# An empty VectorE instruction ahead of each unit's product, more scan inputs made by TensorE, and a one-element minimum in another form

## The chip, the cores and the metric

The kernel runs on one core of one Trainium2 chip. The metric is the device time of one execution in microseconds (us); lower is better. Times given as a median come from three runs; the profile is of one further execution.

## What is computed

All arithmetic is in float32. The input `x` has 4 images of 384 channels and 32 x 32 positions (L = 1024). Layer 0 normalises over groups of channels and applies a four-direction selective scan; layer 1 is causal attention and a mixture of four experts with top-2 gates. The reference, cut to what matters here:

```python
# layer 0, per image and direction k (rows, columns, and both reversed)
x_dbl = einsum('bkdl,kcd->bkcl', xs, x_proj_weight)       # dts (12), Bs (16), Cs (16)
dt = softplus(einsum('bkrl,kdr->bkdl', dts, dt_projs_weight) + bias)
h = h * exp(dt * A) + (dt * u) * B                         # along l, 16 states for each channel
y = sum over states of h * C
x = x + gelu(layernorm(merge(y + D * u)))
# layer 1, tokens t of each image
t = t + softmax(causal(q k^T * scale)) v
t = t + sum over experts e of gate_e * (gelu(xn w1_e + b1_e) w2_e + b2_e)
```

## The kernel before, in words

The scan is cut into **units**: a unit is 32 channels x 4 states (128 partitions) by 1024 positions. An image has 192 units (3 blocks of channels, 4 directions, 4 sets of states, 4 parts of 32 channels), the kernel 768. Four units that follow each other (one set of states, all 128 channels) make a **group**. `IMAGE` is 192, `NJ` is 4, `NU` is 768.

A unit needs these steps, each by one helper:

- `decay` (L548, instruction at L552): ScalarE computes da = exp(dt * A). `dap` has three buffers, so the decay of unit n waits for the scan of unit n - 3.
- `front` (L556, L559): VectorE multiplies dt*u by B, both spread over 128 partitions in SBUF, and writes v to PSUM.
- `middle` (L561, L565): VectorE's scan h = h * da + v, with da in SBUF and v in PSUM. The pool of h has seven buffers.
- `back` (L570, L572): GpSimd multiplies h by C in place. It is given a dependency on the v product of the next unit, so that it runs beside a scan.
- `row` (L578, L597): TensorE sums the states of a group's four units into y by matmuls with a selection matrix.

In image 0, where TensorE has no attention or expert work yet, `feed` (L776) prepares some groups in another way: TensorE transposes dt*u (L815), ScalarE scales it by B (L838, 32 small instructions for a group), and `turned` (L852, L860) lets TensorE transpose the result into PSUM as v; such a unit has no `front`. `scaled` holds the prepared groups; the pool `st` has two buffers, and a group that would come too late is left out.

The order of all work is written by hand in one loop over a clock (L1393 on), one step per unit. In step t it issues the decay of unit t + 2, deferred work, `front(t)`, `turned(t + 1)`, `back(t - 1)`, more deferred work (`inner`), `middle(t)`, the row of the group that ended at t - 2, loads, a piece of the preparation of a coming image, and then TensorE work of attention and experts of an earlier image, with a budget of 4.4 us (attention) or 3.3 us (experts) for each step (`go_on`, L1364). Work is cut up by generators that yield ("wait", n) to go on n steps later, or ("pe", us) to charge their budget. Each engine runs its instructions in the order in which they were issued; a layer above adds the semaphore waits that the buffers need.

`preparation(b)` (L481) normalises an image and computes the projections; the preparation of image b + 1 runs beside the scan of image b, so those of images 0 and 1 fall in the steps of image 0. `project_dt` (L409) makes dt for two directions and one block of channels, in two halves of 512 positions: matmuls (L425), a step of waiting (L429), softplus on ScalarE (L431); then it stores dt to DRAM, multiplies by u on VectorE (L439) and stores the product.

`attention` (L942) handles 128 query rows at a time. `softmax` (L1008) takes the minimum over one or two pieces of the negated scores (L1014), combines two pieces with L1016, and lets ScalarE take the exponential (L1018); `normalise` (L1025) adds the two partial sums (L1028). `experts` (L1184) runs its matmuls at L1260 and L1285, moves the first to SBUF on ScalarE (L1245), applies gelu (L1249), and adds the second's result on VectorE (L1294, L1297), which frees its bank of PSUM.

The functions that the diff touches, and what calls them:

Of the kernel before, what the change touches and what calls it, by code (L numbers as in the profile page):

```python
# [10 lines left out]
ALU = mybir.AluOpType  # L11
# [22 lines left out]
NQ = N // NI  # L34
# [8 lines left out]
AHEAD = 5  # L43
# [6 lines left out]
def hybrid_kernel(  # L50
# [358 lines left out]
    def project_dt(b, pair, m, u, xd):  # L409

        ks = PAIRS[pair]
        while not slots.ready(3 + pair):
            yield "wait", 1
        v = u[m]
        if pair == 1:
            v = slots.now(f"ut_{b}_{m}", P, L)
            nc.scalar.copy(v.rearrange("p (w h) -> p w h", h=HW), columns(u[m]))
        dts = [slots.now(f"dt_{b}_{k}_{m}", P, L) for k in ks]
        for h in range(NH):
            while not banks.ready(2):  # L420
                yield "wait", 1
            pss = [banks.now(f"pdt_{b}_{k}_{m}_{h}") for k in ks]
            for i, k in enumerate(ks):
                r = slice(64 * pair + 32 * i, 64 * pair + 32 * i + R)
                nc.tensor.matmul(  # L425
                    pss[i], wdt[r, m * P : (m + 1) * P], xd[r, bass.ts(h, 512)],
                    start=True, stop=True,
                )
            yield "wait", 1  # L429
            for i, k in enumerate(ks):  # L430
                nc.scalar.activation(  # L431
                    dts[i][:, bass.ts(h, 512)], pss[i], AF.Softplus, bias=dtb[:, k, m : m + 1]
                )
                banks.give(f"pdt_{b}_{k}_{m}_{h}")
        yield "wait", 1
        for i, k in enumerate(ks):
            nc.sync.dma_start(dts_d[b, k][0, m * P : (m + 1) * P, :], dts[i])
            du = yield from slots.take(f"du_{b}_{k}_{m}", P, L)
            nc.vector.tensor_mul(du, dts[i], v)  # L439
            yield "wait", 1  # L440
            nc.sync.dma_start(dts_d[b, k][1, m * P : (m + 1) * P, :], du)
            if b == 0:
                stored_du.add((k, m))
            slots.give(f"dt_{b}_{k}_{m}", f"du_{b}_{k}_{m}")
        if pair == 1:
            slots.give(f"ut_{b}_{m}")
# [101 lines left out]
    def decay(n):  # L548
        u = units[n]
        u["da"] = dap.tile([P, L], F32, tag="da", name=f"da_{u['name']}")  # L550
        g = u["k"] * NG + u["m"] * NJ + u["j"]
        nc.scalar.activation(  # L552
            u["da"], spread["dt4", n], AF.Exp, scale=a4[:, g, u["q"] : u["q"] + 1]
        )

# [5 lines left out]
    def middle(n):  # L561
# [5 lines left out]
            op0=ALU.mult, op1=ALU.add,  # L567
        )

    def back(n, after):  # L570
        h = units[n]["h"]
        product = nc.gpsimd.tensor_tensor(h, h, spread["bc", n][:, 1, :], ALU.mult)  # L572
        order(product, after, mybir.DependencyClass.Sync, "beside a scan")

    ys = {}
# [2 lines left out]
    def row(n):  # L578

        u = units[n]  # L580
        b, m = u["b"], u["m"]
        first = u["pair"] == 0 and u["i"] == 0 and u["q"] == 0
        last = u["pair"] == 1 and u["i"] == 1 and u["q"] == NQ - 1
        if first:
            ys[b, m] = ps_y.tile([P, L], F32, tag="y", name=f"y_{u['name']}")
        for half in range(NH):
            for jj in range(NJ):
                h = units[n - NJ + 1 + jj]["h"]
                y = ys[b, m][jj * DJ : (jj + 1) * DJ, bass.ts(half, 512)]
                if u["pair"] == 0:  # L590
                    h = h[:, bass.ts(half, 512)]
                else:

                    h = h.rearrange("p (w h) -> p w h", h=HW)
                    h = h[:, :, half * HW // 2 : (half + 1) * HW // 2]
                    y = columns(y)
                nc.tensor.matmul(  # L597
                    y, sel, h, start=first, stop=last, tile_position=(0, jj * DJ)
                )
        if last:  # L600
            defer(2, lambda: evict(b, m), inner)
        elif u["pair"] == 1 and u["i"] == 1 and u["q"] == 0:
            side.append(skip(b, m))
# [172 lines left out]
    def feed():  # L776
        bt = one.tile([P, 2, NT, 4 * N], F32, tag="fx0", name="bt")

        def turn_rows(pair):
            while pair not in stored_rows:  # L780
                yield "wait", 1
            rows = yield from slots.take(f"bt_{pair}", 4 * N, L)
            nc.sync.dma_start(rows, rows_d[0, pair].rearrange("k j n l -> (k j n) l"))
            yield "wait", 2
            ps = yield from banks.take(f"pbt_{pair}")
            for t in range(NT):
                nc.tensor.transpose(
                    ps[:, t * 4 * N : (t + 1) * 4 * N], rows[:, t * P : (t + 1) * P],
                    ident[: 4 * N, : 4 * N],
                )  # L790
            yield "wait", 1
            nc.scalar.copy(bt[:, pair], ps.rearrange("p (t n) -> p t n", t=NT))
            banks.give(f"pbt_{pair}")
            slots.give(f"bt_{pair}")

        begun = []
        yield from turn_rows(0)
        for n in range(0, IMAGE, EACH):
            u = units[n]
            if clock[0] > n + EACH - NJ - AHEAD:  # L800
                continue
            if u["pair"] == 1 and u["m"] == 0 and u["i"] == 0:
                yield from turn_rows(1)
            while (u["k"], u["m"]) not in stored_du:
                yield "wait", 1
            name = f"turn_{u['name']}"
            du = yield from slots.take(name, P, L)
            nc.sync.dma_start(du, dts_d[0, u["k"]][1, u["m"] * P : (u["m"] + 1) * P, :])
            yield "wait", 2

            def dut(q, h, du=du, name=name):
                ps = banks.now(f"{name}_{q}_{h}")
                for t in range(4):
                    o = (4 * h + t) * P
                    nc.tensor.transpose(ps[:, t * P : (t + 1) * P], du[:, o : o + P], ident)  # L815
                return ps

            for q in range(1, NQ, 2):
                n0 = n + q * NJ
                if clock[0] > n0 - AHEAD:  # L820
                    continue
                while len(begun) >= 2 and clock[0] < begun[-2] + NJ:

                    yield "wait", 1
                if clock[0] > n0 - AHEAD:
                    continue
                begun.append(n0)
                st = pools["st"].tile([P, NT, NJ * P], F32, tag="st", name=f"st_{n0}")
                ps = [None, None]
                for h in range(2):  # L830
                    if ps[h] is None:
                        while not banks.ready():
                            yield "wait", 1
                        ps[h] = dut(q, h)
                        yield "wait", 1
                    for t in range(4):
                        for i in range(NI):
                            nc.scalar.activation(  # L838
                                st[:, 4 * h + t, :].rearrange("p (d i) -> p i d", i=NI)[:, i, :],
                                ps[h][:, t * P : (t + 1) * P], AF.Copy,  # L840
                                scale=bt[:, u["pair"], 4 * h + t, u["i"] * 2 * N + q * NI + i :][:, :1],
                            )
                        if t == 1:
                            if h == 0 and banks.ready():
                                ps[1] = dut(q, 1)
                            yield "wait", 1
                    banks.give(f"{name}_{q}_{h}")
                    yield "wait", 1
                scaled[n0] = st
            slots.give(name)  # L850
# [91 lines left out]
    def attention(b, yb, fx0):  # L942
# [65 lines left out]
        def softmax(i, ss, pr):  # L1008
# [4 lines left out]
            for n, (o, e, ps) in enumerate(ss):  # L1013
                nc.vector.tensor_reduce(nb[:, n : n + 1], ps, AX.X, ALU.min)  # L1014
            if len(ss) == 2:
                nc.vector.tensor_tensor(nb[:, 0:1], nb[:, 0:1], nb[:, 1:2], ALU.min)  # L1016
            for n, (o, e, ps) in enumerate(ss):
                nc.scalar.activation(  # L1018
                    pr[:, o:e], ps, AF.Exp, bias=nb[:, 0:1], scale=-1.0,
# [5 lines left out]
        def normalise(i, nb, n):  # L1025
            wd = (i + 1) * P
            if n == 2:
                nc.vector.tensor_add(nb[:, 2:3], nb[:, 2:3], nb[:, 3:4])  # L1028
            nc.vector.reciprocal(nb[:, 2:3], nb[:, 2:3])
            nc.scalar.activation(prs[i][:, :wd], prs[i][:, :wd], AF.Copy, scale=nb[:, 2:3])  # L1030

# [361 lines left out]
    while t < NU + 4 or waiting or side or due or inner or parked:  # L1393
# [5 lines left out]
        if t == IMAGE:  # L1399
            second()  # L1400
            side.append(fold())
        done = None
        if t < NU and "v" not in units[t]:
            done = front(t)
        if t + 1 < IMAGE:
# [71 lines left out]
```

## Time and profile before

| what | value |
| --- | --- |
| median of three runs | 3781.38 us (3779.78 to 3781.87) |
| profiled execution: time, span | 3782.19 us, 3780.4 us |
| mean granted TensorE clock | 0.926 |
| first scan of image 0, 1, 2, 3 starts at | 50.3, 682.9, 1511.4, 2331.6 us |
| last scan starts at | 3112.0 us |
| busy in the span: PE, DVE, ACT, POOL | 3348.6, 2962.4, 2088.0, 1815.4 us |
| L565 scan, 768 of them | 1750.6 us busy, 2284 ns each |
| L559 v product, 678 | 840.6 us busy, 1240 ns each |
| L572 product on GpSimd, 768 | 1814.3 us busy, 2367 ns each |
| L552 decay, 768 | 882.8 us busy, 1156 ns each |

PE is TensorE's matmuls and PEld its weight loads, DVE is VectorE, ACT ScalarE, POOL GpSimd, SP the queue that issues DMAs. A line like L565 is the line of the kernel that issued the instruction. The views used are: the page (busy shares, and 40 slices of the span with busy tenths), the timeline (start, duration, engine, line, operation, and in brackets the idle time in front with what ended it), groups of instructions by line (busy us, mean ns of one, idle in front), and tables of busy time in stretches. Ends of matmuls are modelled, and one profile entry stands for half of a program's float32 matmul.

### The profile page before, as it was taken

What the parts mean: (1) busy time and instruction counts of PE and PEld (TensorE: products, weight loads), DVE (VectorE), ACT (ScalarE), POOL (GpSimd) and SP (SyncE); (2) the same over time, 40 slices, a digit from 0 to 9 for tenths busy, and PEclk for the clock granted to TensorE, in tenths of its full rate; (3) what the DMA queues carried; (4) which work ended last, traced back from release to release, by engine and by line L of the source; (5) the groups of instructions that cost most, each with busy time, mean ns of one, the idle gap of its engine ahead of it and who ended that gap; (6) DMA issues with size and microseconds to landing.
All of it is one profiled execution on the core that took longest, in us unless ns stands there. A gap on an engine that the chain in (4) does not pass through costs nothing. (4 is left out here: it accounts for less than half of the span.)

```text
span 3780.4 us, 34707 instructions
## 1 busy us (share of the span) xinstructions
PE 3348.6 (89%) x11755; PEld 1523.6 (40%) x11755; DVE 2962.4 (78%) x2098; ACT 2088.0 (55%) x2754; POOL 1815.4 (48%) x776
## 2 busy tenths in 40 slices
PE   4666666689999999799999999889999998999999
PEld 1333323345343334345333344454344334644444
DVE  5899899988899899989988999999999992210000
ACT  5888888555666556556655555455554552322121
POOL 2777777545466556545555565455665660000000
PEclk7777876799999999898999999899999999999999
DMA  6656555635676757436666655455667551322321
GB/s 202 221 211 223 203 210 200 235 141 177 211 247 210 253 197 245 152 136 219 218 218 227 203 201 197 143 172 196 209 197 241 178 182 38 91 78 81 97 82 53
DMA packets 408017, 680.01 MB, mean 180 GB/s; under 512 B 33520, under 2 KB 279968, under 8 KB 407840
## 3 DMA queue, kind: packets, MB, share of 16 engines
q1 hardware_dynamic: 401632, 677.40, 52.6%
q8 instruction: 93, 1.52, 0.2%
q10 hardware_dynamic: 6208, 0.39, 0.1%
q14 instruction: 84, 0.69, 0.1%
HBM read 605.16 MB, written 72.55 MB: 179 GB/s over the span
## 5 line engine op out<-in xcount | busy, mean ns | idle before, releaser
L572 POOL TENSOR_TENSOR h<-h,bc 128x1024 f32<-128x1024 f32 x768 | 1814.3, 2367 | 1300.8 <-DVE v L559 1170.4
L565 DVE TENSOR_TENSOR_SCAN h<-da,v 128x1024 f32<-128x1024 f32 x768 | 1750.6, 2284 | 107.2 <-PE v L860 31.8
L552 ACT ACTIVATE da<-dt,a 128x1024 f32<-128x1024 f32 x768 | 882.8, 1156 | 916.0 <-DVE h L565 877.8
L1260 PE MATMUL ph<-fx,w 128*128 128x512 f32 x2304 | 1023.3, 600 | 3.5 <-DMA w<-in_w 2.0
L1285 PE MATMUL fy<-ht,w 128*128 128x512 f32 x2304 | 1022.4, 601 | 1.7 <-ACT dt L431 0.9
L559 DVE TENSOR_TENSOR v<-du,bc 128x1024 f32<-128x1024 f32 x678 | 840.6, 1240 | 35.0 <-DMA du<-dts 18.3
L1285 PEld LDWEIGHTS fy<-ht,w 128*128 128x128 f32 x2304 | 437.1, 192 | 575.9 <-issue 558.9
L1260 PEld LDWEIGHTS ph<-fx,w 128*128 128x128 f32 x2304 | 433.8, 191 | 578.6 <-issue 532.8
L597 PE MATMUL y<-h,sel 128*32 128x512 f32 x3072 | 489.7, 659 | 97.4 <-POOL h L572 97.2
L1245 ACT ACTIVATE ht<-ph,b1s 128x512 f32<-128x512 f32 x384 | 257.5, 678 | 463.3 <-PE ph L1260 462.5
L1294 DVE SCALAR_TENSOR_TENSOR fy<-fy,b2s,tw 128x512 f32<-128x512 f32 x96 | 72.4, 754 | 423.0 <-PE fy L1285 423.0
L597 PEld LDWEIGHTS y<-h,sel 128*32 128x32 f32 x3072 | 97.6, 116 | 407.4 <-issue 219.0
L860 PE MATMUL v<-ident,st 128*128 128x128 f32 x720 | 144.2, 366 | 112.7 <-DVE h L565 111.6
L838 ACT ACTIVATE st<-turn,bt 128x128 f32<-128x128 f32 x736 | 213.6, 532 | 0.1
L860 PEld LDWEIGHTS v<-ident,st 128*128 128x128 f32 x720 | 116.1, 190 | 158.3 <-DVE h L565 77.9
L1249 ACT ACTIVATE ht<-ht 128x3072 f32<-128x3072 f32 x64 | 176.9, 2764 | 0.8
L552 ACT ACT_TABLE_LOAD x108 | 138.6, 1283 | 15.5 <-DMA dt<-dts 11.8
L1067 PE MATMUL po<-pt,vt 128*128 128x256 f32 x480 | 110.2, 383 | 10.1 <-ACT pt L959 10.0
L425 PE MATMUL pdt<-xd,wdt 12*128 12x512 f32 x184 | 78.9, 753 | 33.4 <-ACT dt L431 24.7
L997 PE MATMUL ss<-axn,qt 128*128 128x512 f32 (+3 forms) x288 | 101.3, 497 | 7.7 <-ACT yb L1084 6.4
L1067 PEld LDWEIGHTS po<-pt,vt 128*128 128x128 f32 x480 | 96.0, 204 | 27.8 <-ACT pt L959 13.1
L997 PEld LDWEIGHTS ss<-axn,qt 128*128 128x128 f32 x288 | 50.5, 193 | 50.2 <-issue 30.0
(208 smaller groups left out, 1618.3 us busy)
## 6 DMA issues: line engine op xcount, KB each, us to landing
bc<-rows SPq DMA_DIRECT2D x384, 512.0 KB, 4.7
w<-in_w SPq DMA_DIRECT2D x384, 384.0 KB, 5.9
dt<-dts SPq DMA_DIRECT2D x192, 512.0 KB, 3.9
du<-dts SPq DMA_DIRECT2D x192, 512.0 KB, 6.5
dts<-dt SPq DMA_DIRECT2D x48, 512.0 KB, 3.6
dts<-du SPq DMA_DIRECT2D x48, 512.0 KB, 3.8
fx<-t2d SPq DMA_DIRECT2D x12, 768.0 KB, 5.8
tw<-mkd SPq DMA_DIRECT2D x32, 256.0 KB, 6.5
```

The costliest lines, as they stand in the source:

```text
L552: nc.scalar.activation(u["da"], spread["dt4", n], AF.Exp, scale=a4[:, g, u["q"] : u["q"] + 1])
L559: return nc.vector.tensor_tensor(u["v"], spread["du4", n], spread["bc", n][:, 0, :], ALU.mult)
L565: nc.vector.tensor_tensor_scan(u["h"][:, ::step], u["da"][:, ::step], u["v"][:, ::step], 0.0, op0=ALU.mult, op1=ALU.add,)
L572: product = nc.gpsimd.tensor_tensor(h, h, spread["bc", n][:, 1, :], ALU.mult)
L597: nc.tensor.matmul(y, sel, h, start=first, stop=last, tile_position=(0, jj * DJ))
L838: nc.scalar.activation(st[:, 4 * h + t, :].rearrange("p (d i) -> p i d", i=NI)[:, i, :], ps[h][:, t * P : (t + 1) * P], AF.Copy, scale=bt[ ...
L860: nc.tensor.transpose(u["v"][:, t * P : (t + 1) * P], st[:, t, u["j"] * P : (u["j"] + 1) * P], ident)
L1067: nc.tensor.matmul(pv[:, o:], vt[:, j, m * P : (m + 1) * P], pts[step][j // 4][:, j % 4, o:], start=(alone and j == 0), stop=(j == nj - 1),)
L1245: nc.scalar.activation(ht[:, f, :], ps, AF.Identity, bias=bias)
L1249: nc.scalar.activation(ht, ht, AF.Gelu)
L1260: nc.tensor.matmul(ps, tiles[n][:, c, (f % 2) * P : (f % 2 + 1) * P], xns[h][:, c, :], start=(c == 0), stop=(c == M - 1),)
L1285: nc.tensor.matmul(pss[m], tiles[n][:, f, :], hts[fh][:, f, :], start=(fh == 0 and f == 0), stop=(fh == 1 and f == FH - 1),)
```

## The change

Four edits.

1. In `project_dt`, the second half's step of waiting between matmul and softplus is left out while the clock is in image 0.
2. In `feed`, the groups prepared for TensorE are no longer every second one: of each five groups, numbered from the start of the image, those with remainder 1, 3 and 4 are.
3. The two combining instructions on one element for each partition (L1016, L1028) are written as tensor_scalar with the second operand as a per-partition scalar, in place of tensor_tensor.
4. From image 1 on, each step issues an empty VectorE instruction ahead of `front`. It is given dependencies on the unit's decay, and in the last unit of a group also on the product and the last row matmul of the unit four before. `decay`, `back` and `row` note their instructions for it.

```diff
@@ project_dt
-            yield "wait", 1
+            if h == 0 or clock[0] >= IMAGE:
+
+                yield "wait", 1
@@ decay
-        nc.scalar.activation(
+        u["decay"] = nc.scalar.activation(
@@ new, after middle
+    def ahead(n):
+
+        wait = nc.vector.engine_nop()
+        after = [units[n]["decay"]]
+        if n % NJ == NJ - 1 and n > NJ:
+
+            after += [units[n - NJ]["product"], units[n - NJ]["row"]]
+        for x in after:
+            order(wait, x, mybir.DependencyClass.Sync, "ahead of the product")
@@ back
-        product = nc.gpsimd.tensor_tensor(h, h, spread["bc", n][:, 1, :], ALU.mult)
+        product = units[n]["product"] = nc.gpsimd.tensor_tensor(h, h, spread["bc", n][:, 1, :], ALU.mult)
@@ row
-                nc.tensor.matmul(
+                units[n]["row"] = nc.tensor.matmul(
@@ feed
-            for q in range(1, NQ, 2):
+            for q in range(NQ):
                 n0 = n + q * NJ
-                if clock[0] > n0 - AHEAD:
+                if n0 // NJ % 5 not in (1, 3, 4) or clock[0] > n0 - AHEAD:
                     continue
@@ softmax
-                nc.vector.tensor_tensor(nb[:, 0:1], nb[:, 0:1], nb[:, 1:2], ALU.min)
+                nc.vector.tensor_scalar_min(nb[:, 0:1], nb[:, 0:1], nb[:, 1:2])
@@ normalise
-                nc.vector.tensor_add(nb[:, 2:3], nb[:, 2:3], nb[:, 3:4])
+                nc.vector.tensor_scalar_add(nb[:, 2:3], nb[:, 2:3], nb[:, 3:4])
@@ the loop over the clock
         done = None
+        if IMAGE <= t < NU:
+            ahead(t)
         if t < NU and "v" not in units[t]:
             done = front(t)
```

## The prediction

> **What bounds the kernel now.** I read the page first: busy shares, then slices.
>
> ```profile
> PE 3348.6 (89%) x11755; PEld 1523.6 (40%) x11755; DVE 2962.4 (78%) x2098; ACT 2088.0 (55%) x2754; POOL 1815.4 (48%) x776
> DVE  5899899988899899989988999999999992210000
> ```
>
> VectorE's 78% is an average over two stretches. Its slices stand at 8 and 9 until slice 33 (up to about 3120 us), then fall to nearly nothing: from there on the chain of what ended last holds little but TensorE matmuls (L1260, L1285). All edits lie before that tail or leave it alone, so what VectorE gains before 3112 us (the last scan's start) shifts the tail, if nothing else ends later. From VectorE's timeline I took the idle stretches over 0.2 us: 34 us in 62 to 660 us, of which 31 are a scan waiting for TensorE's L860, and 94 us in 660 to 3140. So VectorE is the bound of all four images. How a unit spends it shows in the timeline of a quiet stretch (start, duration, engine, line):
>
> ```profile
> 2800.84 1.23 DVE L559 TENSOR_TENSOR v<-du,bc 128x1024 f32<-128x1024 f32 x1
> 2802.21 2.29 DVE L565 TENSOR_TENSOR_SCAN h<-da,v 128x1024 f32<-128x1024 f32 x1
> 2804.53 1.23 DVE L559 TENSOR_TENSOR v<-du,bc 128x1024 f32<-128x1024 f32 x1
> 2802.25 2.35 POOL L572 TENSOR_TENSOR h<-h,bc 128x1024 f32<-128x1024 f32 x1 [1.34 <-DVE v L559]
> ```
>
> The period is 3.69 us: product 1.23, gap 0.14, scan 2.29, gap 0.03. The 0.14 precedes a scan that waits for several engines; the 0.03 precedes a product whose last wait is for VectorE itself. GpSimd's product starts 0.18 after v ends and ends 0.07 into the next v.
>
> TensorE is close behind, by the view of stretches (the columns after the length are PE, PEld, DVE, ACT and POOL busy, clock, DMA share, GB/s):
>
> ```profile
> 62.00:660.00 598.00, 381.18 (x1750) 186.07 (x1751) 551.80 (x311) 501.87 (x1033) 433.88 (x183) 0.73 0.59 210
> 1050.00:1200.00 150.00, 150.00 (x457) 60.36 (x456) 144.47 (x92) 97.80 (x94) 88.42 (x38) 1.00 0.67 230
> 1500.00:1650.00 150.00, 131.03 (x544) 58.77 (x537) 134.77 (x90) 81.35 (x93) 75.39 (x32) 0.93 0.44 154
> 2850.00:3000.00 150.00, 149.33 (x454) 59.73 (x453) 144.36 (x92) 79.95 (x75) 90.15 (x39) 1.00 0.67 227
> ```
>
> In the expert stretches TensorE is busy 149 to 150 of 150 us; in the attention stretch it has 19 us to spare.
>
> [...]Over all products that begin while GpSimd's still runs by more than 0.14 us, the end is 1.09 us after GpSimd's end (1.36 us when 0.27 remained, 1.60 at the worst), and the minimum over one element, L1016, takes ten times as long beside GpSimd as in the tail:
>
> ```profile
> 825.79 1.71 DVE L1016 TENSOR_TENSOR nb<-nb 128x1 f32<-128x1 f32 x1
> 3220.22 0.16 DVE L1016 TENSOR_TENSOR nb<-nb 128x1 f32<-128x1 f32 x1
> ```
>
> [...]an instruction that waits for several engines may get separate semaphore instructions in front. In the built program the scans of the last three images have up to two; VectorE's fall from 1456 to 720 and 576 empty instructions come in. [...]No line of before shows its time.
>
> **The change part by part.**
>
> *Image 0, units by TensorE.* The built order has 104 scans fed by TensorE in place of 90, in 26 full groups of four. One TensorE-fed and one ordinary group take 24.0 us together (scan starts 447.50 and 471.51); ordinary units there run at 3.65 us (products end at 450.91, 454.52, 458.21, 461.85), so a fed one costs (24.0 - 4 x 3.65) / 4 = 2.35. Fourteen units move: 14 x 1.30 = 18 us less VectorE. ScalarE pays three groups of 32 scalings, 9.1 us each (eight take 2.28), so 27 us, and TensorE 136 short matmuls, with slack (381 of 598 busy).
>
> *Image 0, the left-out wait.* The second half's softplus follows its matmul in the same step, beside the first half's. The page of this stretch has 20 table loads at each of two lines:
>
> ```profile
> L431 ACT ACT_TABLE_LOAD x20 | 25.7, 1283 | 0.3
> L552 ACT ACT_TABLE_LOAD x20 | 25.7, 1283 | 0.4
> ```
>
> The built program has 20 fewer loads there: 20 x 1.283 = 25.7 us, which pays for the 27. The new cost: ScalarE stands at the softplus until TensorE's matmul is done, about 1.1 us in each of 11 calls, with the decays (L552) behind it; they are made two units ahead, which covers it. The stores to DRAM are issued one step earlier on SP, at the same distance from their softplus, and no DMA is added. ScalarE stays near 502 + 27 - 26 + 12 = 515 of some 580 us: room on average, but two fed groups now follow each other (groups 3 and 4 of five) and their scalings crowd into one ordinary group of 14.6 us, which holds 4 x 1.15 of decays and at most one set of 9.1. I take 15 us; ends 3 and 18.
>
> *The small minimum and sum.* Twelve L1016 lie beside GpSimd, 16.4 us in all; at 0.16 each they'd be 1.9. [...]L1028 takes 0.13 already. These lie in attention stretches, where TensorE has room and softmax follows. I take 10.
>
> *The empty instruction.* It takes the waits for ScalarE (every unit) and for TensorE and GpSimd (one unit in four). Behind it stand v, the expert sums (L1294, L1297) that free PSUM for TensorE, the scan, and through v GpSimd's product of the unit before. I compared, in the timelines, the end of each y row (L597) with the start of the v that would now wait for it: of 143 rows the median one ends 4.1 to 6.3 us earlier, by stretch, and seven end later, by 7 us together. Decays are ready about 6 us before. So the moved wait costs at most some 5 us, where TensorE is late anyway.
> The scan then waits for VectorE alone and starts 0.03 after v: 0.10 less, in the 450 units of the last three images where it directly follows v. Not all of it counts: GpSimd's product ends no earlier, and the next v can't end before 1.09 us after it. That cycle is 0.18 + 2.36 + 1.09 = 3.63, and image 0's ordinary units run at 3.65 by just this rule. With 3.64 the gain is 0.045 x 450 = 20 us.
> Its own cost c comes 576 times. From below: zero, hidden, since an independent instruction starts 0.09 before the recorded end of a scan and v 0.03 after it, a window of 0.12. From above: independent tiny instructions stand 0.14 to 0.18 apart (L340 and L341), so 0.06 inside the window, 0.18 if nothing hides it. I take 0.02: nothing under the lock's cover in the 450 units (3.58 + 0.02 is still below 3.64), 2 us in the other 126.
> Then TensorE is late next. Of the 450 units some 285 lie in expert stretches, 13 of the 20 us; there TensorE has 21.6 us idle in 3 x 450 (1050, 1800 and 2550 onwards), and in the last a backlog: the closing L617 waits 11.3 us for y. Half of 13 and most of the attention's 7: 12 us. ScalarE's added self-waits (some 330 semaphore instructions) are covered by its 45% of idle time.
>
> Sum: 15 + 10 + 12 = 37. The profiled execution has a span of 3780.4 and a time of 3782.2; it becomes 3743 and 3745. Against the median 3781.4: **3744 us**.
>
> **The rivals.**
> - *[...]ScalarE's crowding eats image 0:* either leaves 37 - 10 or 37 - 15, both 12: 3754 to 3769. For it: [...]image 0's present 31 us of waits for L860. Against: ScalarE's idle 90.9 us behind scans there.
> - *GpSimd's lock doesn't hold the cycle:* then 0.10 x 450 = 45 less a few, with TensorE's slack used up: 15 + 14 + 37 = 66, 3715. Against: the 1.09 rule.
> - *Slower: the empty instruction is not hidden.* It enters VectorE only once the scan has ended, and v behind it. A direct unit takes 3.58 + c against 3.685, the other 126 take c more. With 25 us from the other edits the balance is 450 x (c - 0.105) + 126c = 25, c = 0.126 us. At c = 0.16: 25 + 20 - 25 = +20, 3801.
> - *It doesn't do what it says:* the built order excludes this; every scan after image 0 keeps at most its wait for VectorE.
>
> **How the numbers follow.** Forecast (3730 to 3757) 0.50; the first rival 0.20; no lock 0.13; slower 0.12; a mixture within 0.2% (7.6 us, about what a measurement of this kernel can tell from no change) 0.05. Faster 0.83, same 0.05, slower 0.12. Range 3715 to 3785: it leaves out the slower case and a few per cent below.
>
> **What would show it.** Right: scans 0.03 after v, a period near 3.64, products with durations up to 1.27[...], L1016 near 0.16, 20 table loads fewer before 660 us, image 0 about 15 us shorter, and in expert stretches TensorE at 150 of 150. Wrong: a gap before v well over 0.05 (the empty instruction costs), L1016 still above 1 us, scans of image 0 waiting longer for L860 or L552, or v held behind late y rows.

## The result, and the profile after

The changed kernel takes 3748.93 us in the median of four runs (3744.69 to 3751.91), the kernel before 3781.28 us (four runs). The ratio is 0.9912, 95% interval 0.9899 to 0.9924: 32.4 us less, where 37 were forecast. The profiled execution has a span of 3745.0 us and a time of 3747.1.

The first lines of the page and VectorE's row of slices, of the kernel after:

```profile
PE 3350.6 (89%) x11891; PEld 1529.0 (41%) x11891; DVE 2961.6 (79%) x2084; ACT 2085.8 (56%) x2832; POOL 1817.8 (49%) x776
DVE  5999899988998998989998999999999982210000
```

VectorE's busy time is what it was (2962.4 before), although it has 14 products fewer and 12 shorter minima. So the 35 us of span did not come off its busy time as a whole: some durations fell and others rose. The timeline shows which. This is the quiet stretch again, after the change (start, duration, engine, line; the last line is GpSimd's):

```profile
2800.04 2.29 DVE L567 TENSOR_TENSOR_SCAN h<-da,v 128x1024 f32<-128x1024 f32 x1
2802.36 1.26 DVE L561 TENSOR_TENSOR v<-du,bc 128x1024 f32<-128x1024 f32 x1
2803.66 2.29 DVE L567 TENSOR_TENSOR_SCAN h<-da,v 128x1024 f32<-128x1024 f32 x1
2805.98 1.26 DVE L561 TENSOR_TENSOR v<-du,bc 128x1024 f32<-128x1024 f32 x1
2800.18 2.36 POOL L584 TENSOR_TENSOR h<-h,bc 128x1024 f32<-128x1024 f32 x1 [1.26 <-DVE v L561]
```

The scan now follows v after 0.03 to 0.04 us (2803.66 - 2802.36 - 1.26 = 0.04) where it was 0.13 to 0.14, and v follows the scan after 0.03 as before, in spite of the empty instruction between them (VectorE's 2098 instructions stand in the profile before in the order in which the program issues them). But v takes 1.26 where it took 1.23: GpSimd's product ends at 2802.54, and v ends 1.08 later, at 2803.62. So it is wherever a v product begins with more than 0.14 us of a GpSimd product left: 119 do before and 440 after, and they end 1.08 to 1.10 us after GpSimd's end, 1.09 in the median of each kernel. This holding is what the prediction calls the lock; what in the hardware makes it is not shown. The period is 3.62 (3.69 before).

The two single-element forms, before in the first two lines and after in the third (groups by line: count, then busy us, mean ns of one):

```profile
L1016 DVE TENSOR_TENSOR nb<-nb 128x1 f32<-128x1 f32 x16 | 17.1, 1066 | 0.5
L1028 DVE TENSOR_TENSOR nb<-nb 128x1 f32<-128x1 f32 x16 | 2.2, 137 | 5.4 <-ACT pr L1018 5.4
```
```profile
L1028 DVE TENSOR_SCALAR nb<-nb 128x1 f32<-128x1 f32 x16 | 3.4, 214 | 0.6
```

(L1028 of the kernel after is the minimum that was L1016.) All sixteen now take 0.21 us, with GpSimd at work (eleven of them) or not.

In image 0 the lines of ScalarE and VectorE between 62 and 660 us, after:

```profile
L554 ACT ACT_TABLE_LOAD x11 | 14.1, 1283 | 0.2
L433 ACT ACT_TABLE_LOAD x10 | 12.8, 1283 | 0.2
L433 ACT ACTIVATE dt<-pdt,dtb 128x512 f32<-128x512 f32 x40 | 25.4, 685 | 18.2 <-PE pdt L425 18.1
```
```profile
L441 DVE TENSOR_TENSOR du<-dt,x 128x1024 f32<-128x1024 f32 x10 | 18.0, 1804 | 3.7 <-ACT dt L433 3.7
```

The table loads are halved as forecast (20 and 20 before). What is new: ScalarE stands 18 us for the projection's matmul (0.7 before), and ten of the products dt*u take 1804 ns each, where the same ten took 1272.

Where the time went, by image, from the starts of scans 0, 192, 384, 576 and 767 in VectorE's timeline:

| us | image 0 | image 1 | image 2 | image 3 | after the last scan |
| --- | --- | --- | --- | --- | --- |
| before | 632.6 | 828.5 | 820.2 | 780.5 | 668.4 |
| after | 625.0 | 820.4 | 811.3 | 771.5 | 666.5 |

### The profile page after: what moved, and what is told of

It reads as the page before. It is cut to its first block, busy times and chain, and to the rows that moved or that the text cites. A ratio compares the mean times of both kernels' runs of the same rounds, so it can differ in the third digit from the quotient of the medians.

```text
span 3745.0 us, 35189 instructions
## 1 busy us (share of the span) xinstructions
PE 3350.6 (89%) x11891; PEld 1529.0 (41%) x11891; DVE 2961.6 (79%) x2084; ACT 2085.8 (56%) x2832; POOL 1817.8 (49%) x776
## 5 line engine op out<-in xcount | busy, mean ns | idle before, releaser
L567 DVE TENSOR_TENSOR_SCAN h<-da,v 128x1024 f32<-128x1024 f32 x768 | 1748.4, 2283 | 48.4 <-PE v L872 17.3
L850 ACT ACTIVATE st<-turn,bt 128x128 f32<-128x128 f32 x832 | 244.2, 554 | 0.0
L872 PEld LDWEIGHTS v<-ident,st 128*128 128x128 f32 x832 | 121.7, 175 | 127.7 <-DVE h L567 74.2
L425 PE MATMUL pdt<-xd,wdt 12*128 12x512 f32 x184 | 88.0, 813 | 45.7 <-ACT dt L433 22.6
L1079 PEld LDWEIGHTS po<-pt,vt 128*128 128x128 f32 x480 | 90.4, 192 | 22.3 <-ACT pt L971 10.1
```

Of the source, the lines that this page charges most:

```text
L567: nc.vector.tensor_tensor_scan(u["h"][:, ::step], u["da"][:, ::step], u["v"][:, ::step], 0.0, op0=ALU.mult, op1=ALU.add,)
L850: nc.scalar.activation(st[:, 4 * h + t, :].rearrange("p (d i) -> p i d", i=NI)[:, i, :], ps[h][:, t * P : (t + 1) * P], AF.Copy, scale=bt[ ...
L872: nc.tensor.transpose(u["v"][:, t * P : (t + 1) * P], st[:, t, u["j"] * P : (u["j"] + 1) * P], ident)
L1079: nc.tensor.matmul(pv[:, o:], vt[:, j, m * P : (m + 1) * P], pts[step][j // 4][:, j % 4, o:], start=(alone and j == 0), stop=(j == nj - 1),)
```

## The experiments

Medians, each beside runs of the kernel before on the same chip. "Minus" is the median's distance from those.

| run | us | minus | ratio, 95% interval |
| --- | --- | --- | --- |
| e1_wait (edit 1) | 3791.33 | -10.0 (slower) | 1.0017 to 1.0030 |
| e12_image0 (edits 1, 2) | 3778.61 | 2.7 | 0.9983 to 0.9999 |
| e3_small (edit 3) | 3769.63 | 11.7 | 0.9954 to 0.9978 |
| e4_empty (edit 4) | 3770.16 | 11.2 | 0.9958 to 0.9981 |
| e34_no_image0 (edits 3, 4) | 3756.86 | 24.6 | 0.9922 to 0.9947 |
| m1_du_first | 3755.41 | 26.1 | 0.9914 to 0.9942 |
| m2_own_image_only | 3745.87 | 36.3 | 0.9886 to 0.9915 |
| c_half_product | 3732.66 | 48.8 | 0.9856 to 0.9883 |
| c_three_empty | 3756.22 | 25.3 | 0.9918 to 0.9945 |
| c_plain_empty | 3781.89 | 0.2 | 0.9988 to 1.0005 |
| light_tensor_before | 3379.48 | - | 0.8916 to 0.8947 |
| light_tensor_e4 | 3357.16 | - | 0.8858 to 0.8885 |

### Image 0: edits 1 and 2

**Edit 1 alone**, the diff of the first edit and nothing else:

```diff
-            yield "wait", 1
+            if h == 0 or clock[0] >= IMAGE:
+
+                yield "wait", 1
```

> Only the left-out step of waiting in project_dt (edit 1). If ScalarE's table loads cost image 0 nothing (VectorE bounds it), 3778 to 3782, within 4 us of before; if they held scans back, 3770 to 3776. Either way some 20 table loads fewer before 680 us.

Measured: 3791.33, 10 us slower; in its profile (3785.9 us, one of its faster executions) image 0 takes 643.7 us, 11.1 more than before, and image 1 takes 823.0, 5.5 less. No expectation had a loss of this size. Edit 2 was not run alone. The second run adds it to edit 1.

> Edits 1 and 2, all that touches image 0. The prediction's sum gives 3766 (15 us less); by the profile after, image 0 gave only 7.6 us, so I now expect 3772 to 3775. If it gives the full 15, the loss in the changed kernel comes from the edits together.

Measured: 3778.61, image 0 at 625.7. Edit 2 on top of edit 1 takes 643.7 - 625.7 = 18.0 us off image 0 in the profiles, and 3791.33 - 3778.61 = 12.7 us off the medians. Where VectorE's time goes with edit 1 is seen in a balance of its timeline over image 0: busy time by kind, gaps up to 0.2 us, and longer ones. The sum of the short gaps can be negative, since an instruction that does not depend on the one before it starts up to 0.09 us before that one's recorded end.

| us, image 0 | scans | v | dt*u | other | short gaps | standing over 0.2 | length |
| --- | --- | --- | --- | --- | --- | --- | --- |
| before | 437.9 | 129.9 | 25.2 | 4.2 | -1.9 | 37.3 | 632.6 |
| e1_wait | 437.8 | 127.7 | 30.3 | 6.4 | -1.5 | 42.9 | 643.7 |
| after | 437.5 | 114.9 | 30.8 | 6.2 | -1.7 | 37.3 | 625.0 |
| m1_du_first | 437.6 | 114.5 | 24.9 | 6.4 | -1.6 | 43.6 | 625.5 |

With edit 1 alone, the products dt*u take 5.1 us more (1.3 of them for one product more within image 0), "other" 2.2, and VectorE stands 5.6 us more. Three places show it. One dt*u product (VectorE, first) begins under three GpSimd products that follow each other (second),

```profile
96.89 3.35 DVE L441 TENSOR_TENSOR du<-dt,x 128x1024 f32<-128x1024 f32 x1 [0.29 <-ACT dt L433]
```
```profile
92.18 6.98 POOL L574 TENSOR_TENSOR h<-h,bc 128x1024 f32<-128x1024 f32 x3 [1.26 <-DVE v L561]
```

and ends at 100.24, 1.08 after GpSimd's end at 99.16. Second, a tensor_tensor on three elements of the group norm takes 2.38 us, 0.16 before (in the changed kernel its neighbour L360 takes 2.22, and ends 0.02 after a GpSimd product that was running when it began); third, v stands longer for the load of dt*u that the preparation stored in DRAM. Groups by line in image 0, before and then with edit 1:

```profile
L359 DVE TENSOR_TENSOR gn_dev<-gn_mc,gn_mean 128x3 f32<-128x3 f32 x1 | 0.2, 163 | 0.0
L559 DVE TENSOR_TENSOR v<-du,bc 128x1024 f32<-128x1024 f32 x102 | 129.9, 1274 | 2.3 <-DMA du<-dts 2.2
```
```profile
L359 DVE TENSOR_TENSOR gn_dev<-gn_mc,gn_mean 128x3 f32<-128x3 f32 x1 | 2.4, 2383 | 0.0
L561 DVE TENSOR_TENSOR v<-du,bc 128x1024 f32<-128x1024 f32 x100 | 127.7, 1277 | 8.7 <-DMA du<-dts 8.3 <-DMA bc<-rows 0.4
```

ScalarE stands at the softplus as the prediction had it. With edit 1 alone (us in total, times, longest, 62 to 660 us):

```profile
ACT dt L433 <- PE pdt L425: 12.7, 13, 2.6
```

VectorE's scans wait only 2.4 us for decays there (0.6 before). Why the load of dt*u comes later was not tried. My explanation for the held products: without the step of waiting, the product comes up on VectorE right behind a softplus that is itself still waiting (the one above stands 0.29 us for it), and starts at a time that nothing keeps clear of GpSimd. To test it I kept the product clear: in the changed kernel, where a dt*u product was issued in the step of a unit fed by TensorE, GpSimd's product of that step waits for it.

```diff
-            nc.vector.tensor_mul(du, dts[i], v)
+            held_by[:] = [nc.vector.tensor_mul(du, dts[i], v)]
@@ back
+        if after is None and held_by:
+            after = held_by.pop()
+        held_by.clear()
```

> The changed kernel; in image 0, GpSimd's product of a unit fed by TensorE also waits for a dt*u product that VectorE was given just before. Theory: in image 0 ten products du<-dt,x take 1.80 us each in place of 1.26[...]; they fall to about 1.25 and image 0 gets 4 to 6 us shorter: 3743 to 3746. Rival: GpSimd is itself close behind in those groups (2.4 us a unit against a scan of 2.28) and hands the delay back: 3748 to 3752.

Measured: 3755.41 (3747.51 to 3756.88), image 0 at 625.5. The products are freed,

```profile
L441 DVE TENSOR_TENSOR du<-dt,x 128x1024 f32<-128x1024 f32 x10 | 12.4, 1240 | 3.7 <-ACT dt L433 3.7
```

and the balance shows the 6 us come back as standing (37.3 to 43.6). So the theory fell: freeing these products by holding GpSimd back gains nothing. What takes the 6 us is not chiefly GpSimd, as the rival had it (scans wait 1.3 us for its products, 0.7 in the changed kernel), but waits for the softplus (5.6 to 8.1 us), for the load of B and C rows (0.9 to 3.8) and for TensorE's transposes into v (17.3 to 19.7). The median lies 6 us over the changed kernel's, outside the rival's range too, but the runs of the two kernels overlap.

The last run on image 0 keeps edit 1 to image 0's own preparation; that of image 1, which lies in image 0's steps too, has its wait back.

```diff
-            if h == 0 or clock[0] >= IMAGE:
+            if h == 0 or b > 0:
```

> The changed kernel with the first edit kept to the preparation of image 0 itself; the preparation of image 1, which runs beside image 0's scan, has its step of waiting back. Theory (in image 0 the first edit costs some 10 us by ScalarE standing at the softplus and by products of dt and u held by GpSimd, as it did alone): ScalarE's wait for pdt in image 0 falls from 18 us to under 8, image 0 gets shorter than 621 us, time 3738 to 3746. Rival (with the other edits in place the first edit costs nothing, since the table loads that it saves pay for the scalings): image 0 at 624 us or longer, time 3748 to 3757.

Measured: 3745.87, image 0 at 631.0. ScalarE's wait for the matmul fell from 18.1 to 8.6 us, but image 0 did not get shorter, and VectorE stands 43.7 us in it. That theory fell, though the median lies just inside its range; in time this kernel and the changed one cannot be told apart (3745.76 to 3749.24 against 3744.69 to 3751.91). So how much of edit 1's loss is left beside the other edits stays open. A caution belongs here: in e34_no_image0, which leaves image 0's code as before, the profile has image 0 at 637.6, against 631 to 633 in six other profiles of that code. Differences of 6 us in image 0 between single profiles prove little; edit 1's loss rests on its 21 timed runs, and edit 2's 18 on two profiles. That the terms of the balance are what causes the loss is not shown: the run that freed the held products gained nothing.

### Edit 3 alone

Its diff is the third edit of the change.

> Only the minimum and the sum as tensor_scalar (edit 3). Theory: [...]14.5 us of VectorE, of which TensorE leaves 10 to 14: 3767 to 3771. Rival: softmax and TensorE set the pace of those steps, then 3777 to 3782.

Measured: 3769.63, 11.7 us less, which is the theory's. In its profile the minima take 3.4 us in all (17.1 before), 212 to 215 ns each, the sums 3.1 (2.2 before): a balance of 12.8, of which nearly all arrives.

### Edit 4: where its gain comes from and where it stops

> Only the empty VectorE instruction (edit 4). Theory: v to scan gap 0.03 and a period of 3.62 where 3.69 was, 450 x 0.065 = 29 us of VectorE, of which TensorE takes about half: 3763 to 3769. Rival: the 26 us that images 1 to 3 gained come from edit 3 and shorter chains of softmax, and the empty instruction gives under 5 us: 3776 to 3781.

Measured: 3770.16, 11.2 us less. The control puts the empty instruction in without its waits:

```diff
+        if IMAGE <= t < NU:
+            nc.vector.engine_nop()
         if t < NU and "v" not in units[t]:
             done = front(t)
```

> The kernel before with one empty VectorE instruction ahead of each product from image 1 on, but without any dependency: the waits for ScalarE, TensorE and GpSimd stay at the scan. Theory (the gain of edit 4 comes from moving the waits away from the scan; the empty instruction itself is hidden): the gap between v and scan stays 0.13 to 0.14, the period in the quiet stretch stays 3.69, the expert blocks of 16 units stay at 62.5 us, time 3779 to 3784. Rival (the empty instruction itself, by what it does to the queue or to the order, brings the gain): gap 0.03, period 3.62, expert blocks 61.7, time near 3770. Rival (it costs something of its own): over 3785.

Measured: 3781.89, no difference. From its timeline of VectorE:

```profile
2805.71 1.23 DVE L559 TENSOR_TENSOR v<-du,bc 128x1024 f32<-128x1024 f32 x1
2807.07 2.29 DVE L565 TENSOR_TENSOR_SCAN h<-da,v 128x1024 f32<-128x1024 f32 x1
2809.40 1.23 DVE L559 TENSOR_TENSOR v<-du,bc 128x1024 f32<-128x1024 f32 x1
```

The gap ahead of the scan is 2807.07 - 2805.71 - 1.23 = 0.13, as before. So it is where the waits stand that makes the gain, not the instruction. The record shows the waits themselves. Part of the scan's waits are separate semaphore instructions in front of it: in images 1 to 3 of the kernel before, the 18 scans for which the profile shows one semaphore to wait for have none, the 558 with two to six have one to three. In the profile they have a row of their own (DVEq is VectorE's sequencer; ns: least, median, greatest), the scan's before and then in e4_empty:

```profile
L565 DVEq EVENT_SEMAPHORE  x1089: 21/49/621, 50.3 to 3111.9; - x182
```
```profile
L565 DVEq EVENT_SEMAPHORE  x220: 21/50/629, 49.3 to 689.3; - x110
```

In images 1 to 3, 449 scans follow their v directly in each kernel. Before, every one of them has one or two semaphore instructions in front and starts 0.13 us after v in the mean, with one as with two; in e4_empty 447 have none and start 0.034 after it. The control still has all 1089. Whether the same waits put on v itself, without an empty instruction, would do as well was not tried.

What the empty instruction costs shows when there are three of them for each unit, in the changed kernel:

```diff
         wait = nc.vector.engine_nop()
+        nc.vector.engine_nop()
+        nc.vector.engine_nop()
```

> The changed kernel with two more empty instructions for each unit, without dependencies. Theory: an empty instruction passes through in the 0.12 us between the end of a scan and the start of v: gap before v 0.03 to 0.06, period at most 3.65, 3746 to 3758. Rival: each takes a place of 0.06 us or more on VectorE that shows: period 3.70 or more, 3790 or more.

Measured: 3756.22 (3753.61 to 3758.28), some 7 us over the changed kernel's 3748.93 for 1152 more instructions (the two ratios' intervals overlap). Scans in the quiet stretch start at 2802.87, 2806.50 and 2810.11, a period of 3.62 still, and 16 units of the expert stretches take 61.8 and 61.7 us as in the changed kernel. The profile's row for one of the three empty instructions in that run:

```profile
L574 DVEq ENGINE_NOP  x576: 1/13/16, 673.6 to 3083.6; - x192
```

Short gaps in images 1 to 3 show where two more of them cost. Where v follows a scan (some 470 times) the gaps sum to 16.6 us with one and with three. Where it follows another instruction (90 times) they go from -5.6 to -0.6 us, 0.055 us a time: these 5.0 us are most of the 6.7 by which the three images are longer. So the empty instruction is hidden behind a scan, and not quite elsewhere.

Next the lock. In the changed kernel GpSimd multiplies only the first half of the positions, so that its product ends before the next v begins; the second half of h goes on without its factor C.

```diff
-        product = units[n]["product"] = nc.gpsimd.tensor_tensor(h, h, spread["bc", n][:, 1, :], ALU.mult)
+        product = units[n]["product"] = nc.gpsimd.tensor_tensor(h[:, :512], h[:, :512], spread["bc", n][:, 1, :512], ALU.mult)
```

> The changed kernel with GpSimd's product over the first 512 of 1024 positions only; the second half of h is left without its factor C. Theory: GpSimd's lock sets the period of 3.62; without it v takes 1.23 and the period is 1.23 + 0.03 + 2.29 + 0.03 = 3.58, 450 x 0.04 = 18 us less at most in images 1 to 3, and image 0's ordinary units fall from 3.65 to 3.6: 3727 to 3742. Rival: VectorE's own chain with the empty instruction sets 3.62, so v stays near 1.26 or the gap before v is 0.06: 3745 to 3750.

Measured: 3732.66, another 16.3 us less. v is back at its old length (groups by line):

```profile
L561 DVE TENSOR_TENSOR v<-du,bc 128x1024 f32<-128x1024 f32 x664 | 816.6, 1230 | 68.3 <-DMA du<-dts 20.7
```

In images 1 to 3 v takes 708.6 us in all where it takes 726.8 in the changed kernel: the lock costs 18 us there. VectorE's standing rises by 8.3 (84.4 to 92.7), and 12.7 come off these images in the profile.

Last, TensorE. In the prediction it takes half of edit 4's gain in the expert stretches and leaves most of it in the attention stretches. By the profiles, with the stretches that the prediction names (from 1050, 1800 and 2550 us to the end of the image), edit 4 took 0.4, 4.4 and 4.3 us off the expert parts of images 1, 2 and 3, and 0.6, 0.3 and 0.7 off the rest. Blocks of 16 units of image 2, in order, show more:

| us | 1 | 2 | 3 | 4 | 5 | 6 | 7 | 8 | 9 to 12 |
| --- | --- | --- | --- | --- | --- | --- | --- | --- | --- |
| before | 74.5 | 78.8 | 72.4 | 70.4 | 65.4 | 70.7 | 65.3 | 73.9 | 62.5, 61.3, 62.5, 62.5 |
| e4_empty | 74.1 | 78.7 | 72.7 | 70.3 | 64.8 | 71.3 | 65.1 | 72.2 | 62.2, 60.6, 61.8, 61.7 |
| light_tensor_before | 74.5 | 67.5 | 73.5 | 70.4 | 65.4 | 67.1 | 64.7 | 68.5 | 62.5, 61.3, 62.5, 62.5 |
| light_tensor_e4 | 74.0 | 67.2 | 74.2 | 69.8 | 64.7 | 66.6 | 64.0 | 68.5 | 61.8, 60.5, 61.7, 61.6 |

Blocks 9 to 12 are expert work with no preparation beside it (the last dt*u product starts at 2048 us, in block 8). The quiet stretch's 0.065 us for each unit, times the 13 of 16 whose scan follows its v directly, would be 0.8, and 0.7 to 0.8 arrive in three of the four. Blocks 1 to 8, where the preparation, the attention and the first expert work lie, gave back most of theirs. So did image 1, where dt*u products run on into block 9 (1315 us); image 3 has none, and its expert part kept 4.3. The light kernels test who takes it; the first two lines of the diff stand for four places (queries and keys, values, scores, the experts' first product):

```diff
-                for c in range(M):
+                for c in range(1):
@@ experts, second product
-                for f in range(FH):
+                for f in range(0, FH, 3):
```

> The kernel before with less TensorE work: of the three matmuls over channels in the queries, keys, values and scores, and in the experts' first product, only the first is done, and of the six in the experts' second product two. So attention and experts are computed from a third of their sums; everything on the other engines stays. It is the base for the next run and tells what TensorE's share of the expert stretches holds up: if VectorE bounds those stretches, the images' lengths up to the last scan fall by under 10 us each and the tail after the last scan (668 us) by over half; if TensorE bounds them, the images fall by 20 us or more each.

> The fourth edit alone (the empty instruction with the moved waits) on the kernel with the lightened TensorE of the run before: attention and experts are computed from a third of their sums. Theory (a unit is 0.065 us shorter wherever the scan directly follows its product, and what the full kernel lacks of 450 x 0.065 = 29 us is taken by TensorE, which is late next): the difference between this run and the light kernel before is 22 to 30 us. Rival (what is lacking is taken by something else, softmax chains, decays or the moved wait): the difference stays at 9 to 14 us, as between the full kernels (11.2).

Measured: 3379.48 and 3357.16, so edit 4 is worth 22.3 us there, twice what it is in the full kernel and at the lower end of what the theory had. In the base the images took 631.1, 800.7, 800.3 and 774.6 us (1.5, 27.8, 19.9 and 5.9 less than before), and the tail 318.0: neither case of its expectation as a whole. TensorE holds VectorE up in images 1 and 2, by 9.8 and 9.7 us in their expert parts too, but not in blocks 9 to 12 of image 2, which stay at 62.5 though two thirds of TensorE's expert work is gone, nor in the expert part of image 3 (0.4 us of 559). Stretches of the two kernels before, full (first) and light:

```profile
2850.00:3000.00 150.00, 149.33 (x454) 59.73 (x453) 144.36 (x92) 79.95 (x75) 90.15 (x39) 1.00 0.67 227
```
```profile
2850.00:3000.00 150.00, 102.44 (x250) 27.58 (x250) 144.08 (x91) 81.77 (x78) 91.55 (x39) 0.81 0.63 215
```

TensorE was busy 149 of 150 us, VectorE 144, and with TensorE at 102 VectorE is still at 144. My reading, which no run tests, is that a full TensorE there works off a backlog that ends in the tail; in the kernel before VectorE has no wait over 0.2 us in this stretch.

The balance of VectorE over images 1 to 3 (first scan of image 1 to the last scan) closes the account:

| us, images 1 to 3 | scans | v | other | short gaps | standing over 0.2 | length |
| --- | --- | --- | --- | --- | --- | --- |
| before | 1313.8 | 709.5 | 287.5 | 44.5 | 73.8 | 2429.1 |
| e4_empty | 1313.5 | 727.3 | 286.9 | 2.8 | 87.7 | 2418.2 |
| light_tensor_before | 1314.0 | 709.3 | 288.1 | 43.7 | 20.5 | 2375.6 |
| light_tensor_e4 | 1313.6 | 725.0 | 289.7 | 2.5 | 24.5 | 2355.4 |
| after | 1313.3 | 726.8 | 274.6 | 4.1 | 84.4 | 2403.2 |

Edit 4 takes 41.7 us of short gaps away. The lock takes 17.8 back, as longer v. Standing takes 13.9 more, and 41.7 - 17.8 - 13.9 = 10.0 of the 10.9 by which the length fell. In the light pair the first two are nearly the same (41.2 and 15.7) and standing takes 4.0. Who is waited for, in e4_empty and then in light_tensor_e4 (us in total, times, longest):

```profile
DVE nb L1024 <- PE ss L1012: 17.8, 7, 9.2
DVE du L439 <- PE ph L1270: 16.1, 3, 8.9
DVE du L439 <- PE fy L1295: 15.8, 4, 8.2
DVE v L559 <- PE y L607: 10.5, 9, 3.7
```
```profile
DVE du L439 <- PE ph L1270: 6.6, 2, 5.8
DVE du L439 <- PE fy L1295: 3.2, 2, 2.4
DVE du L439 <- ACT dt L431: 2.2, 1, 2.2
DVE nb L1024 <- PE ss L1012: 2.2, 2, 1.7
```

The fourth line of the first is the moved wait itself: v stands 10.5 us for late y rows, nine times, where before the row was needed only a product later. With a light TensorE it isn't among the waits. The other three lines stood in the kernel before with much the same sums (22.6, 16.8, 13.9).

### Edits 3 and 4 together

> Edits 3 and 4 without 1 and 2. If the edits add up: 3781.3 - 11.7 - 11.2 = 3758, image 1 near 820 us, images 2 and 3 near 812 and 774. If what the changed kernel has beyond the sum of its parts (7 us) comes from 3 and 4 helping each other: 3750 to 3753. If it comes from 1 and 2 with 4: 3757 to 3760.

Measured: 24.6 us less; 11.7 and 11.2 make 22.9, so the two add up. It leaves 32.4 - 24.6 = 7.8 for edits 1 and 2 beside them, where alone they are worth 2.7. By their intervals each of these medians is uncertain by 3 to 5 us, so that 2.7 and 7.8 are compatible; that edits 1 and 2 gain by the company of the others isn't shown.

## Why the prediction was right, and where it was not

- **What bounds the kernel** was right: VectorE's path shortened, and the tail after the last scan hardly changed (668.4 to 666.5).
- **Edit 4, the mechanism** was right: gap 0.03, the empty instruction hidden behind a scan, v held to 1.26 by GpSimd's lock, period 3.62 for 3.64. The sum of 12 measured 11.2, but by other terms: 23.9 us for VectorE alone (41.7 - 17.8) where 20 stood, and some 13 to 14 lost where 8 stood. That two errors cancel is luck.
- **Edit 4, TensorE "late next"** failed in its place. The prediction took TensorE's 149 to 150 of 150 us in the expert stretches as a bound near by, had half of 13 us arrive there and most of 7 in the attention stretches. The runs showed 9.1 us in the expert parts and 1.6 in the rest, and between expert parts with TensorE nearly equally full (98 to 99%) a spread from 0.4 (image 1) to 4.4 (image 2). What decides is whether VectorE waits for a result of TensorE; it does at the scores (L1014), at the dt*u products (L439, put down to the experts' matmuls) and, since the change, ahead of v for the y rows. That last term was put at "at most some 5 us", though the prediction's own comparison had 7 us of late rows, and measured 10.5; v held behind late y rows is one of the prediction's signs of being wrong. Why it grew from 7 to 10.5 was not tried; a unit which comes earlier would meet the same late row sooner.
- **Edit 3** was right and a little small: 10 taken, 11.7 measured. The new form is not held by GpSimd (0.21 us in the eleven that lie beside its product); no trace of the kernel before shows that, and in the prediction it was an estimate of mine. Nearly the whole of the 12.8 us stood on VectorE's path. The first rival's other case, that the new form is held like the old one and 37 - 10 is left, fell.
- **Edit 2's** 18 us came out as 18.0 in image 0 of the profiles, above edit 1, but as 12.7 between the medians. The agreement is chance: with edit 1 alone 100 units have a `front`, so edit 2 moved 12 more (to 88), and not the 14 of the sum; at the prediction's 1.30 us each that is 15.6. Its rival, that ScalarE's crowding eats image 0, didn't come: in the changed kernel scans wait 17.3 us there for TensorE's transposes, where they waited 31.8.
- **Edit 1** is the step that failed. The prediction took it to pay for the scalings and to cost VectorE nothing; alone it costs 10 us. What the prediction named was right: ScalarE's standing, put at about 12 us, is 12.7 with edit 1 alone (18.1 with edit 2), and scans waited only 1.8 us more for decays. The terms that were missing are VectorE's (image 0 grows by 11.1 us in the profile): the dt*u products behind the late softplus fall under GpSimd's and are held there, a small product of the group norm too, and v waits longer for dt*u from DRAM (8.3 us for 2.2), though the prediction had the stores no later. Which of them makes the loss stays open. The saved table loads (26 us) lie on ScalarE, which has room; of VectorE's waits only that for TensorE's transposes (L860 before, L862 here) fell with them, from 31.8 to 26.6 us. So edits 1 and 2 gave 3 alone and about 8 beside the others, not 15; with edit 3's and edit 4's 23 to 25 that is the measured 32.
- **The slower rival** (c from 0.126 us) is excluded by c_plain_empty (no difference) and by the run with three. The rival without a lock is excluded by v at 1.26; c_half_product, which takes most of the lock away, brings 16 of the 25 us that this rival had over the forecast for edit 4.

## What to carry to other kernels

Where two instructions of one engine follow each other in a tight loop, look at the gap ahead of each: here a wait that was long fulfilled (the decay ends 8.3 us ahead of its scan in the median of images 1 to 3 before) still cost 0.10 us when it stood on the scan, whose input had just been made by the same engine, and nothing that shows one instruction earlier, behind the scan before (a gap of 0.03 us with the waits and without). Before counting the gain, look at which lock or late result comes next, and add the gaps, durations and waits of the engine in a balance like the ones above: it shows at once how much each gave back. In this kernel an engine at 149 of 150 us was a bound on another only where the other waited for it.

## What the runs showed of the hardware

- In this kernel a one-element minimum with its second operand as a per-partition scalar takes 0.21 us, the same beside GpSimd's product as in the tail; as tensor_tensor it took 0.16 in the tail and 0.67 to 1.71 beside GpSimd. Without a GpSimd product in the way the new form is the slower one: the sums, which never met one, went from 137 to 196 ns.
- A scan that follows its own-engine input directly starts 0.13 us after it with one or two separate semaphore instructions in front, and 0.034 without (449 scans in each kernel).
- An empty VectorE instruction is recorded in the sequencer's row at 13 ns in the median (1 to 16), and three of them between a scan and the next product leave the period at 3.62 us; ahead of a product that follows something else, two more cost 0.055 us.
- The v and dt*u products (128x1024) that begin with more than 0.14 us of a GpSimd product left end 1.08 to 1.10 us after that one's end (140 of them before, 455 after), whether they lost 0.03 us by it (v, 1.26) or 2.1 (dt*u, 3.35).
- With two thirds of its attention and expert matmuls gone, TensorE was granted a mean clock of 0.806, against 0.926 in the full kernel.
